# A list scheduler with other distances between engines, other GpSimd durations and other constants

## The chip, the core and the metric

The kernel runs on one core of a Trainium2 chip. The metric is the device time of one execution in microseconds (us). Of the kernel before, 15 runs are known, from 796.47 to 799.75, with a median of 798.31. One further execution was recorded by the hardware profiler.

The engines are named as in the profile: PE (TensorE, matrix products, with PEld for the loading of its weights), DVE (VectorE), ACT (ScalarE), POOL (GpSimd) and SP (SyncE, whose queue issues most of the DMA transfers). Each engine works through its own list of instructions in order. An instruction that isn't ready holds up all that stand behind it on its engine.

## The reference

Two layers run over x (4 sequences of 1024 tokens, 128 features), each with a layernorm over its sum with x:

```python
# selective state space layer: 256 channels, 16 states
xz = x @ W_in.T                       # xr, z
xs = silu(causal_conv(xr, 4 taps) + conv_b)
dt_r, b_sel, c_sel = split(xs @ W_x.T)
dt = softplus(dt_r @ W_dt.T + b_dt)
h  = exp(dt * a) * h + (dt * x_t) * b_t          # token after token
y  = sum_s h * c_t + D * x_t
x  = layernorm(x + (y * silu(z)) @ W_out.T)
# mixture of 8 experts, the best 2 of each token
scores = x @ Wr + br; weights = softmax(top 2)
out = sum over experts of weight * (gelu(x @ W1 + b1) @ W2 + b2)   # 128 -> 512 -> 128
x   = layernorm(x + out)
```

The program computes all of it in float32.

## The kernel before, in words

**Units and states.** The 4096 tokens are cut into ten units (`UNITS`, L42) of 256, 256, 512 (six times), 384 and 128 tokens, numbered 0 to 9. Each unit runs through 16 states s, and a state is one pass over the unit's tokens for all 256 channels, which lie as two halves c of 128 partitions. Here a state is called "S4.9" or "state 9 of unit 4". It takes these steps in `step`:

- PE spreads the column of B over the partitions (tile u, L824, at most 4 transposes);
- DVE multiplies, u = dtx * u (L861), and runs two scans along the tokens, h = a*h + u (L880, first c = 1, then c = 0);
- ACT makes a = exp(dt * nega) for the scans (L847, 7 buffers);
- POOL multiplies hc = h * cc, a half at a time (L895), and copies the last column of h as the state of the next unit of the same sequence (L920), where the sequence goes on. SP loads cc, the row of C for all partitions;
- PE adds hc, transposed, to y (L905).

h has 2 buffers, hc 3, cc 4. So the scan of a state waits until POOL has made hc of the state two before it.

**Around the states.** While unit i runs, `prepare(i+1)` makes the next one's xs, zs, dt and dtx (projections L585 to L721, DVE's q L753, dt L766, dtx L780). `finish_mixer` closes unit i during unit i+1: yg = y * zs on DVE (L959), transposes py on PE (L973) with copies yt on ACT (L980), the output projection po on PE (L991, L1002), the layernorm (stats_m L466 and mv_m L468 on DVE, rstd_m on ACT and DVE), the transposes pt_f (L1027) and the copy xf (L1031), the router's product pr (L1036), and on DVE the scores sc (L1057), the ranks (L1071 to L1077) and the weights rw (L1098 to L1101).

**Experts.** The tokens of a round (`ROUNDS`, L45: units 0 and 1, then each unit to 8 by itself, as rounds 0 to 7) are sorted by expert into blocks of 128 slots, 15 in a round, 13 in round 7. `dispatch` counts on PE (L1140, L1149), numbers the blocks on DVE (L1174 to L1193), finds each token's slot (L1202 to L1220) and its weight (L1233, L1241), and then POOL scatters the rows into `xs_slots` by indirect DMA (L1262), two for each 128 tokens: 8 of them, 6 in round 7. `experts` loads four blocks at a time (xb, L1332), transposes them on PE (pt_b, L1343), makes xq on ACT or DVE (L1350, L1359), multiplies by the expert's weights w (loaded by SP, L1402) on PE (L1290), takes the GELU on ACT (ht, L1303), multiplies by the second weights (L1314), weighs yb on ACT or DVE (L1426, L1428) and stores it (L1435). `combine` adds the biases (L1461, L1473), gathers the rows back on POOL (L1495), and does the last layernorm (stats_o L466, o L492) and the store (L1524). Unit 9 isn't sorted; all 8 experts run over its 128 tokens (`dense`, L1532 to L1564).

**What sets the order.** Nothing above is issued as it is written. Each operation is added to a `Plan` (L77 to L248) with an engine, a cost in us, what it reads and writes, a place (a due time) and an urgency. `order` is a list scheduler: on each engine it takes, among the operations that could start within NEAR of the earliest, that with the lowest place less urgency. An operation is known to be ready when all that it needs has ended, plus a hop when that ran on another engine (`HOP`, L81). Other rules: a buffer must be free; an ACT operation that needs another function table counts LOTH later than it could start, unless its urgency is RUSH, and 1.28 for the switch; DVE operations marked `port` and POOL's hc aren't planned at the same time; POOL's scatters and gathers (`beside`) are put next to DVE work by BESIDE and PATIENCE. What `order` returns is issued in that order on each engine, and `issue` adds a load of ACT's function table where the next operation needs another one (L243). The costs and places shape the order alone; on the chip each instruction starts when its engine and its data are there.

The places come from the constants of L19 to L40. `prepare` of unit i is due PREP + PREP_OF[i] before its start, the dispatch of round r at the end of its last unit plus D_AT + D_OF[r], the experts X_AT + X_OF[r], the combining C_AT + C_OF[r] behind. `finish_mixer` has the urgency URG, or RUSH in the last N_RUSH units (L952).

Of the kernel before, what the change touches and what calls it, by code (L numbers as in the profile page):

```python
# [16 lines left out]
NTC = T // P  # L17

RUSH = 100.0  # L19
NEAR, LOTH = 0.1, 1.3  # L20

UP = 0.95
GATHER, SCATTER = 1.85, 1.35
N_B = 2
SCAN_ORDER = 1, 0
B_AT, B_URG = 3.6, 29.9
BESIDE = -6.2
PATIENCE = 0.2
N_RUSH = 0
X_AT, X_STEP, X_URG, C_AT, C_URG, D_AT = 1.9, 2.66, 6.2, 4.0, -1.0, -1.9  # L30
A_AT, A_URG, BC_AT, BC_URG = -0.8, -2.3, 4.2, 15.8
PREP, SEL, SOFT, SSTEP = 25.4, 5.3, -0.1, 2.7
L_URG = -1.0
URG, URG2, URG3, URG4 = 52.0, 191.1, 18.3, 0.8
Z_AT, W2_AT, W1_AT, W1_STEP = 11.2, 0.0, 6.8, 3.5

PREP_OF = (-6.7, -1.0, -10.0, 9.5, 1.2, 0.0, -3.0, 5.6, -5.2, 6.9, -3.9, 3.0)
D_OF = (7.9, -3.5, -6.5, 3.3, 6.5, 4.7, -8.1, 5.3, 4.5, 1.7)
X_OF = (-1.9, -7.6, 2.1, 1.3, 0.5, 0.4, 0.8, -16.1, 6.0, -2.5)
C_OF = (-0.2, 5.0, -3.5, -1.3, 8.3, 3.3, 21.1, -2.6, 2.7, 9.1)  # L40

UNITS = [  # L42
    (0, 0, 256), (0, 256, 256), (0, 512, 512), (1, 0, 512), (1, 512, 512), (2, 0, 512), (2, 512, 512), (3, 0, 512), (3, 512, 384), (3, 896, 128),
# [33 lines left out]
class Plan:  # L77

    HOP = {"PE": 0.3, "DVE": 0.12, "ACT": 0.15, "POOL": 0.15}  # L81

    def __init__(self):
        self.ops, self.room, self.place = [], {}, 0.0
# [62 lines left out]
    def order(self, near=0.1, switch=1.28, loth=1.3, ahead=60.0, free_tags=("mm",)):  # L147
# [13 lines left out]
        while ready:  # L161
# [5 lines left out]
            for op in ready:  # L167
# [17 lines left out]
                if op["beside"] and needy:  # L185
                    if port[0] == "DVE" and max(t, port[1]) <= port[2] - BESIDE:
                        t = max(t, port[1])
                    else:
                        t = max(t, known + PATIENCE)
                s = t  # L190
# [61 lines left out]
def tile_mamba_moe_postln(  # L252
# [171 lines left out]
    def size(i):  # L424
        return UNITS[i][2], UNITS[i][2] // P
# [376 lines left out]
    def step(i, st, s):  # L802
        t_n, n = size(i)
        b, first, _ = UNITS[i]
        goes_on = i + 1 < NU and UNITS[i + 1][0] == b
        if s == 0 and first == 0:
            state[b] = sb(small, [P, NS, NDC], "state", 2, f"state_{b}")
        carry = state[b]
        place = plan.place
        cc = sb(scan, [P, T], "cc", 4, f"cc_{i}_{s}")  # L810
        cd, bt, dt, dtx = st["cd"], st["bt"], st["dt"], st["dtx"]
        turn = turns[0]
        bank = 2 * (turn % N_B)
        turns[0] += 1
        spreads[turn], users[turn] = [], []
        begun[turn] = plan.buf(None, 1, None)
        to_spread = lambda ins: apart(spreads[turn], ins, users.get(turn - 1, ()))
        to_use = lambda ins: apart(users[turn], ins, spreads.get(turn + 1, ()))
        row = plan.buf("row", N_B, lambda: u_sb[:, bank, :])

        def spread():
            for k in range(n):
                to_spread(
                    nc.tensor.transpose(  # L824
                        u_sb[:, bank, k * P : (k + 1) * P],
                        bt()[:, k, s : s + 1].to_broadcast([P, P]),
                        ident,
                    )
                )


        late = [begun[turn - 1]] if turn else []
        pe(0.12 * n, spread, [bt, *late], [row], place=place - B_AT, urgent=B_URG)
        dma(
            lambda: nc.sync.dma_start(
                out=cc()[:, :t_n], in_=cd()[s, :t_n].partition_broadcast(P)
            ),
            [cd],
            [cc],
            t_n // 2,  # L840
            place=place - BC_AT,
            urgent=BC_URG,
        )
        a = sb(scan, [P, NDC, T], "a", 7, f"a_{i}_{s}")
        act(
            2 * t_n,
            lambda: nc.scalar.activation(  # L847
                a()[:, :, :t_n], dt()[:, :, :t_n], AF.Exp, scale=nega[:, s : s + 1]
            ),
            [dt, decay],  # L850
            [a],
            EXP,
            place=place - A_AT,
            urgent=A_URG,
        )
        h = sb(scan, [P, NDC, T], "h", 2, f"h_{i}_{s}")

        dve(
            2 * t_n,
            lambda: to_use(  # L860
                nc.vector.tensor_tensor(  # L861
                    (u_sb[:, 1:3, :t_n] if bank else u_sb[:, 1::-1, :t_n]),
                    dtx()[:, :, :t_n],
                    u_sb[:, bank : bank + 1, :t_n].to_broadcast([P, NDC, t_n]),
                    ALU.mult,
                )
            ),
            [dtx, row],
            [u_first, row, begun[turn]],
            port=False,  # L870
        )
        hc = sb(scan, [P, NDC, T], "hc", 3, f"hc_{i}_{s}")
        if s == 0:
            add_skip(i, st)
        y = st["y"]
        for c in SCAN_ORDER:

            def run(c=c):
                to_use(
                    nc.vector.tensor_tensor_scan(  # L880
                        h()[:, c, :t_n],
                        a()[:, c, :t_n],
                        u_sb[:, (1, bank)[c], :t_n],
                        0.0 if first == 0 else carry()[:, s, c : c + 1],
                        op0=ALU.mult,
                        op1=ALU.add,
                    )
                )

            plan.add(  # L890
                "DVE", (0.21 if first else 0.15) + 2.1e-3 * t_n, run, [(u_first, row)[c], a] + [(carry, s)] * (first > 0), [(h, c)]
            )

            def times(c=c):
                nc.gpsimd.tensor_tensor(  # L895
                    hc()[:, c, :t_n], h()[:, c, :t_n], cc()[:, :t_n], ALU.mult
                )

            plan.add(
                "POOL", 0.05 + 2.33e-3 * t_n, times, [(h, c), cc], [(hc, c)], urgent=30.0, port=True  # L900
            )

            def add(c=c):
                for k in range(n):
                    nc.tensor.matmul(  # L905
                        y()[:, k, c * P : (c + 1) * P],
                        hc()[:, c, k * P : (k + 1) * P],
                        ident,
                        is_transpose=True,
                        start=False,  # L910
                        stop=(s == NS - 1),
                        skip_group_check=True,
                    )

            plan.add("PE", 0.12 * n, add, [(hc, c), y], [y], urgent=30.0)
        if goes_on:
            plan.add(
                "POOL",
                0.15,
                lambda: nc.gpsimd.tensor_copy(carry()[:, s, :], h()[:, :, t_n - 1]),  # L920
                [h],
                [(carry, s)],
                urgent=30.0,
            )
# [24 lines left out]
    def finish_mixer(i, st, at):  # L949
        t_n, n = size(i)  # L950
        plan.place = at
        plan.urgent = URG if i < NU - N_RUSH else RUSH  # L952
        yg = sb(tmp, [P, NTC, DI], "sq", 2, f"yg_{i}")
# [614 lines left out]
    for rd in rounds:  # L1568
        c = 0
# [99 lines left out]
```

## Time and profile before

| | |
|---|---|
| median of 15 runs | 798.31 us (796.47 to 799.75) |
| the profiled execution | 795.18 us |
| its span, first to last instruction | 793.5 us |
| mean granted TensorE clock | 0.913 |
| hc (L895), halves of 512 tokens | 192 of 1.428 us |
| state copies (L920) of this form | 96 of 0.342 us |
| first scans of 512 with a state / without | 1.266 / 1.208 us |
| u (L861) of 512 tokens | 1.227 us |
| ACT table loads (L243) | 105 of 1.283 us |
| rows gathered (L1495) | 62 of 1.579 us |

The page first gives the busy time of each engine, its share of the span and its instructions; then the span in 40 slices with the busy share in tenths. The table of waits names the waiting operation, what it waited for, and the sum, the number and the longest of the waits. A line of the timeline gives start, duration, engine, line, operation, tiles, and in brackets the idle time ahead of it with what ended it; the mean times in the table are those of groups of one shape. Idle time of an engine matters only where its work sets the end.

### The profile page before, as it was taken

What the parts mean: (1) busy time and instruction counts of PE and PEld (TensorE: products, weight loads), DVE (VectorE), ACT (ScalarE), POOL (GpSimd) and SP (SyncE); (2) the same over time, 40 slices, a digit from 0 to 9 for tenths busy, and PEclk for the clock granted to TensorE, in tenths of its full rate; (3) what the DMA queues carried; (4) which work ended last, traced back from release to release, by engine and by line L of the source; (5) the groups of instructions that cost most, each with busy time, mean ns of one, the idle gap of its engine ahead of it and who ended that gap; (6) DMA issues with size and microseconds to landing.
All of it is one profiled execution on the core that took longest, in us unless ns stands there. A gap on an engine that the chain in (4) does not pass through costs nothing. (4 is left out here: it accounts for less than half of the span.)

```text
span 793.5 us, 14284 instructions
## 1 busy us (share of the span) xinstructions
PE 657.4 (83%) x4594; PEld 561.5 (71%) x4594; DVE 656.5 (83%) x1036; ACT 557.8 (70%) x843; POOL 534.2 (67%) x637
## 2 busy tenths in 40 slices
PE   5557838669997999799987996899889988888786
PEld 4446526359875987598766874888678978777785
DVE  1698999999979998999989989999979997985322
ACT  3853855817867886778777888788867876676553
POOL 4356545576656897479938795869787886985604
PEclk9666958869997999899998998899989999999998
DMA  6962313347414664267524733556355555566652
GB/s 198 222 150 54 107 47 107 99 133 230 142 56 132 188 175 119 67 175 182 140 61 134 198 82 113 152 178 161 91 146 173 145 145 174 147 143 180 156 158 46
DMA packets 106120, 109.20 MB, mean 138 GB/s; under 512 B 9640, under 2 KB 72152, under 8 KB 106048
## 3 DMA queue, kind: packets, MB, share of 16 engines
q1 hardware_dynamic: 94384, 99.44, 44.3%
q0 software_dynamic: 11248, 8.33, 6.0%
q8 instruction: 38, 0.62, 0.3%
q10 hardware_dynamic: 416, 0.53, 0.3%
q14 instruction: 34, 0.28, 0.1%
HBM read 87.96 MB, written 18.27 MB: 134 GB/s over the span
## 5 line engine op out<-in xcount | busy, mean ns | idle before, releaser
L895 POOL TENSOR_TENSOR hc<-h,cc 128x512 f32<-128x512 f32 (+3 forms) x320 | 357.7, 1212 | 156.2 <-PE y L905 35.1
L905 PE MATMUL y<-ident,hc 128*128 128x128 f32 x1024 | 173.0, 293 | 48.3 <-POOL hc L895 45.8
L880 DVE TENSOR_TENSOR_SCAN h<-a,state,u 128x512 f32<-128x512 f32 (+3 forms) x192 | 185.4, 1000 | 20.5 <-POOL hc L895 7.3
L847 ACT ACTIVATE a<-dt,nega 128x1024 f32<-128x1024 f32 (+3 forms) x160 | 152.9, 974 | 66.5 <-DVE h L880 60.3
L861 DVE TENSOR_TENSOR u<-dtx,u 128x1024 f32<-128x1024 f32 (+3 forms) x160 | 162.2, 1014 | 22.0 <-PE u L824 9.5
L905 PEld LDWEIGHTS y<-ident,hc 128*128 128x128 f32 x1024 | 124.7, 150 | 77.3 <-POOL hc L895 71.3
L1314 PE MATMUL ph<-w_sb,ht 128*128 x944 | 131.6, 292 | 24.4 <-ACT ht L1303 24.2
L1314 PEld LDWEIGHTS ph<-w_sb,ht 128*128 128x128 f32 x944 | 121.6, 206 | 29.0 <-ACT ht L1303 28.6
L880 DVE TENSOR_TENSOR_SCAN h<-a,u 128x512 f32<-128x512 f32 (+1 forms) x128 | 132.9, 1075 | 10.1 <-POOL hc L895 3.6
L1290 PE MATMUL ph<-xq,w 128*128 128x128 f32 x944 | 125.9, 283 | 15.4 <-DVE pick L1233 3.2
L243 ACT ACT_TABLE_LOAD x105 | 134.7, 1283 | 3.6 <-PEq L1657 1.8
L1290 PEld LDWEIGHTS ph<-xq,w 128*128 128x128 f32 x944 | 116.3, 198 | 21.4 <-issue 6.4
L1495 POOL DMA_INDIRECT acc<-ys_slots,slot_i x62 | 97.9, 1579 | 39.2 <-DMA ys_slots<-yb 22.3
L824 PE MATMUL u<-ident,bt 128*128 128x128 f32 x512 | 89.3, 289 | 10.7 <-DVE h L880 10.7
L1303 ACT ACTIVATE ht<-ph 128x512 f32<-128x512 f32 x118 | 66.0, 597 | 23.5 <-PE ph L1290 22.6
L824 PEld LDWEIGHTS u<-ident,bt 128*128 128x128 f32 x512 | 65.1, 147 | 20.6 <-DVE h L880 13.1
L1426 ACT ACTIVATE yb<-ph,xb 128x128 f32<-128x128 f32 x105 | 37.2, 363 | 46.7 <-PE ph L1314 41.1
L1262 POOL DMA_INDIRECT xs_slots<-acc,slot_i x31 | 34.9, 1126 | 46.9 <-DVE twin L1241 13.2
L613 PE MATMUL pxc<-xt,taps 128*128 128x512 f32 (+3 forms) x160 | 60.2, 524 | 3.5 <-ACT xt L603 2.9
L613 PEld LDWEIGHTS pxc<-xt,taps 128*128 128x128 f32 x160 | 29.4, 199 | 24.8 <-issue 17.5
L745 ACT ACTIVATE sq<-ex,shift 128x1024 f32<-128x1024 f32 (+3 forms) x40 | 38.0, 973 | 7.3 <-DVE q L753 6.8
L1262 POOL DMA_INDIRECT xs_slots<-twin,slot_i x31 | 35.7, 1151 | 6.7 <-issue 5.4
(140 smaller groups left out, 706.3 us busy)
## 6 DMA issues: line engine op xcount, KB each, us to landing
w<-w_dram SPq DMA_DIRECT2D x118, 256.0 KB
cc<-cd SPq DMA_DIRECT2D x96, 256.0 KB
xb<-xs_slots SPq DMA_DIRECT2D x24, 258.0 KB
ys_slots<-yb SPq DMA_DIRECT2D x24, 256.0 KB
cc<-cd SPq DMA_DIRECT2D x32, 128.0 KB
cc<-cd SPq DMA_DIRECT2D x16, 192.0 KB
w_sb<-in_w_dram SPq DMA_DIRECT2D x8, 256.0 KB
w_own<-in_w_dram SPq DMA_DIRECT2D x8, 256.0 KB
```

Of the source, the lines that this page charges most:

```text
L243: load(table)
L613: nc.tensor.matmul(pp()[:, :t_n], taps[:, k, c * P : (c + 1) * P], xt()[:, k : k + t_n], start=(k == 0), stop=(k == KC - 1),)
L824: nc.tensor.transpose(u_sb[:, bank, k * P : (k + 1) * P], bt()[:, k, s : s + 1].to_broadcast([P, P]), ident,)
L847: lambda: nc.scalar.activation(a()[:, :, :t_n], dt()[:, :, :t_n], AF.Exp, scale=nega[:, s : s + 1]),
L861: nc.vector.tensor_tensor((u_sb[:, 1:3, :t_n] if bank else u_sb[:, 1::-1, :t_n]), dtx()[:, :, :t_n], u_sb[:, bank : bank + 1, :t_n].to_bro ...
L880: nc.vector.tensor_tensor_scan(h()[:, c, :t_n], a()[:, c, :t_n], u_sb[:, (1, bank)[c], :t_n], 0.0 if first == 0 else carry()[:, s, c : c + 1],
L895: nc.gpsimd.tensor_tensor(hc()[:, c, :t_n], h()[:, c, :t_n], cc()[:, :t_n], ALU.mult)
L905: nc.tensor.matmul(y()[:, k, c * P : (c + 1) * P], hc()[:, c, k * P : (k + 1) * P], ident, is_transpose=True, start=False, stop=(s == NS - 1),
L1262: ins = nc.gpsimd.indirect_dma_start(out=rd["xs"]()[:, :], out_offset=bass.IndirectOffsetOnAxis(ap=slot_i()[:, k, st["chunk"] + c : st["ch ...
L1290: nc.tensor.matmul(ph()[:, k * P : (k + 1) * P], w()[:, k * P : (k + 1) * P], xt()[:, width], start=True, stop=True, skip_group_check=True,)
L1314: nc.tensor.matmul(py, ht[:, k, :], w2_sb[:, bass.ds(e, 1), k * DM : (k + 1) * DM].rearrange("p o d -> p (o d)"), start=(k == 0), stop=(k ...
L1495: nc.gpsimd.indirect_dma_start(out=acc()[:, c, :DM], out_offset=None, in_=ys()[:, :], in_offset=bass.IndirectOffsetOnAxis(ap=slot_i()[:, k ...
```

## The change

No operation, buffer or dependence is changed. The scheduler's figures are: the hops between engines, POOL's cost of an hc and of a state copy, and nearly all constants that give places, urgencies and the rules for tables and for POOL beside DVE. So the orders on all five engines differ, and the number of ACT table loads, 105 before, is 90 after.

```diff
-NEAR, LOTH = 0.1, 1.3
+NEAR, LOTH = 0.1, 1.6
-GATHER, SCATTER = 1.85, 1.35
+GATHER, SCATTER = 1.65, 1.25
-B_AT, B_URG = 3.6, 29.9
-BESIDE = -6.2
-PATIENCE = 0.2
-N_RUSH = 0
-X_AT, X_STEP, X_URG, C_AT, C_URG, D_AT = 1.9, 2.66, 6.2, 4.0, -1.0, -1.9
-A_AT, A_URG, BC_AT, BC_URG = -0.8, -2.3, 4.2, 15.8
-PREP, SEL, SOFT, SSTEP = 25.4, 5.3, -0.1, 2.7
-L_URG = -1.0
-URG, URG2, URG3, URG4 = 52.0, 191.1, 18.3, 0.8
-Z_AT, W2_AT, W1_AT, W1_STEP = 11.2, 0.0, 6.8, 3.5
+B_AT, B_URG = 5.3, 30.0
+BESIDE = -13.6
+PATIENCE = 0.3
+N_RUSH = 2
+X_AT, X_STEP, X_URG, C_AT, C_URG, D_AT = -1.0, 2.33, 6.9, 4.9, -0.5, 0.9
+A_AT, A_URG, BC_AT, BC_URG = 4.5, 0.2, 2.6, 24.4
+PREP, SEL, SOFT, SSTEP = 25.3, 7.2, 2.6, 3.6
+L_URG = -2.0
+URG, URG2, URG3, URG4 = 49.9, 241.6, 23.0, 3.7
+Z_AT, W2_AT, W1_AT, W1_STEP = 38.1, -3.2, 2.2, 7.5
-PREP_OF = (-6.7, -1.0, -10.0, 9.5, 1.2, 0.0, -3.0, 5.6, -5.2, 6.9, -3.9, 3.0)
-D_OF = (7.9, -3.5, -6.5, 3.3, 6.5, 4.7, -8.1, 5.3, 4.5, 1.7)
-X_OF = (-1.9, -7.6, 2.1, 1.3, 0.5, 0.4, 0.8, -16.1, 6.0, -2.5)
-C_OF = (-0.2, 5.0, -3.5, -1.3, 8.3, 3.3, 21.1, -2.6, 2.7, 9.1)
+PREP_OF = (-6.7, -0.5, -10.6, 3.4, 0.9, -0.2, -3.0, 1.4, -1.9, 4.2, -9.5, 5.6)
+D_OF = (6.1, -9.1, -5.7, 8.1, 5.3, -0.2, -2.2, 9.8, 4.6, 1.2)
+X_OF = (-1.9, -7.6, 8.3, 5.3, -1.3, 2.1, -4.0, -13.7, 11.7, -0.1)
+C_OF = (-0.1, 19.3, -4.2, 0.4, 8.5, 2.2, 12.4, -1.7, 2.7, 9.3)
-    HOP = {"PE": 0.3, "DVE": 0.12, "ACT": 0.15, "POOL": 0.15}
+    HOP = {"PE": 0.5, "DVE": 0.15, "ACT": 0.3, "POOL": 0.6}
-                "POOL", 0.05 + 2.33e-3 * t_n, times, [(h, c), cc], [(hc, c)], urgent=30.0, port=True
+                "POOL", 0.08 + 2.4e-3 * t_n, times, [(h, c), cc], [(hc, c)], urgent=30.0, port=True
-                0.15,
+                0.32,
```

## The prediction

> **What bounds the kernel now.** I read the page's busy times first, then the slices, the instruction groups, the waits of DVE, the windows of the end, and last the timelines of DVE, POOL and PE around single waits.
>
> ```profile
> PE 657.4 (83%) x4594; PEld 561.5 (71%) x4594; DVE 656.5 (83%) x1036; ACT 557.8 (70%) x843; POOL 534.2 (67%) x637
> ...
> DVE  1698999999979998999989989999979997985322
> ```
>
> DVE's row of slices tells three stretches. It is low for about 29 us (loads and the first projection; the first u starts at 29.31), then 8 or 9 nearly throughout, then it falls after 715. In the long middle DVE sets the pace: a state of 512 tokens is one u (1.23 us) and two scans (1.27 + 1.21), which with gaps comes about every 4.1 us. So there time comes only from DVE's idle.
>
> ```profile
> DVE h L880 <- POOL hc L895: 10.9, 3, 6.4
> ...
> DVE u L861 <- PE u L824: 9.5, 9, 3.3
> ...
> DVE sc L1057 <- PE pr L1036: 4.8, 4, 3.0
> DVE h L880 <- POOL state L920: 3.8, 2, 3.4
> DVE stats_m L466 <- PE po L1002: 3.4, 3, 2.0
> ```
>
> These waits of DVE (us, times, longest) are what a new order can remove. Before 714.9 the timeline of DVE holds 9.0 of the u waits (one of 0.29 comes later, the rest are smaller than 0.2), 4.8 + 3.4 = 8.2 for the new layernorm and router, 1.0 for a gathered acc, and 3.59 + 0.85 + 3.36 + 0.5 on POOL: some 26 us. The larger waits of the view (yb, acc, q) lie in the end or the head.
>
> ```profile
> 714.90:735.50 20.60, 17.82 (x134) 15.28 (x134) 10.48 (x37) 12.19 (x28) 10.62 (x21) 1.00 0.65 176
> 735.50:793.50 58.00, 43.64 (x360) 41.29 (x360) 15.59 (x62) 28.00 (x50) 21.70 (x14) 0.95 0.49 119
> ```
>
> These are windows of the end (length, then busy PE, PEld, DVE, ACT, POOL, clock). From the last dispatch (L1174, 714.88) to the last instruction is 78.6 us: 20.67 until the first block of round 7 is transposed (pt_b, 735.55), then 58 of a PE chain, round 7's 13 blocks and 8 dense ones. **So the time is where the last dispatch stands, plus the end behind it.**
>
> **The change, part by part.** No operation changes; only the orders do, and with them the ACT table loads, 105 before and 90 after. The steps are counted in the two listings of each engine's order, priced by rows of before. The constants, the hops (HOP) and the two GpSimd costs are the scheduler's figures and cost no time on the chip. The profiled run took 795.18, its span was 793.5 (1.7 lies around it), 3.1 under the median of 798.31. I sum on the span and add 4.8 at the end.
>
> (1) *Table loads*: 15 x 1.283 (L243) = 19.2 us less on ACT. ACT is 70% busy and DVE waits for it once, for 10.2 in the head, where the order is nearly the same. I take 0 here; the other engines' waits on ACT are in terms 3 and 7. The next ACTIVATE starts as a load ends (the load at 695.50 ends at 696.78, the next starts at 696.80). The Trainium skill ("ScalarE: Activation LUTs", What ACT_TABLE_LOAD costs) adds a drain to each load, about 2.7 us in all; by that estimate ACT would save 40 us, and the sum would be the same.
>
> (2) *The last dispatch stands later.* Before, it follows both scans of state 10 of unit 9; after, it stands between the two scans of state 15. The same router operations stand ahead of it in both. Added ahead of it: u and scans of states 11 to 14, u and one scan of 15. A state of this unit comes every 1.52 us (u at 695.51, 697.03, 698.55), the last part is 0.43 + 0.10 + 0.47: 4 x 1.52 + 1.0 = **+7.1**. It is certain as work, as these states otherwise run behind the dispatch, where they are hidden.
>
> (3) *Router and projection waits* (8.2). PE and ACT work between them is unchanged, but DVE's own work between yg and stats_m, and from mv_m to sc, grows: in unit 5 from 8.1 to 12.1 and 7.0 to 12.4, in unit 4 to sc 7.5 to 10.7. The longest waits are 3.0 and 2.0, so most are covered; unit 2's stretch to sc shrinks (8.4 to 6.8) and unit 8's to stats_m (7.3 to 6.0). Bounds -8.2 and 0; I take **-6**, near the covered end.
>
> (4) *u waits* (9.0). Spreads (L824) move earlier on PE: 53 of 160 had two whole states of y still behind them, now 77. But lumps stay: up to 8.3 us of PE work ahead of one spread after, 5.4 at the longest wait of before (3.34). Bounds -9 and +3 (one more such wait); I take **-4**. The acc wait goes: **-1**.
>
> (5) *Scatters.* GpSimd runs the 8 scatters of a round in one block, and h has two buffers, so the scan two states on waits for the hc behind the block.
>
> ```profile
> 591.04 2.33 DVE L880 TENSOR_TENSOR_SCAN h<-a,u 128x512 f32<-128x512 f32 x2 [3.59 <-POOL hc L895]
> ```
>
> This is round 5's block (577.27 to 589.7, then 1.24 for the hc). DVE work between the last L1241 and the waiting scan was 11.4 there, 10.2 in round 6 (waited 3.36), and 14.6 or more in all rounds before them, without a wait. After: 15.3, 14.6, **7.5**, 14.7, 15.0, 10.1, 7.8. Demand is 0.4 to 1.7 to start, 10.2 to 12.4 for the block, 1.3 for one hc: 12 to 15. Round 2 gets a new wait, 7.5 against 13 = 5.5 (4.8 to 6.3); round 5 keeps about 3.6; round 6 goes from 3.4 to 4.9. **+7**, bounds 0 (scatters fall between hc after all) and +8.
>
> The skill ("SBUF — State Buffer", Who interferes with whom) says that DVE operations with two SBUF inputs lock out GpSimd's reads. In this trace a scatter takes 0.96 to 2.03, and the block took 10.2 while DVE stood and up to 12.4 while it worked. By that rule a wait would shorten its own block, and +7 would be nearer +5 (the two blocks are 2.2 apart). It speaks against any fixed duration for GpSimd, which the new costs are too.
>
> (6) *Unit 8's yg* (L959) comes after, directly behind its last scan with only 1.1 us of DVE work between; hc and y need about 3: **+2** (0 to 2.5). Nine gathers now stand among unit 9's states, 1.58 each beside hc: **+0.5** (0 to 1).
>
> (7) *The end.* The stall after the last scatters goes (only half a scan follows them):
>
> ```profile
> 720.15 1.04 POOL L1262 DMA_INDIRECT xs_slots<-acc,slot_i  x1 [6.41 <-DVE h L880]
> ...
> 728.53 0.85 DVE L880 TENSOR_TENSOR_SCAN h<-a,state,u 128x128 f32<-128x128 f32 x2 [6.42 <-POOL hc L895]
> ```
>
> The block ends at 727.60, 12.7 behind the dispatch; xb's loads are issued from 730.11 to 733.76, and the first pt_b at 735.55 stands behind y, yg and py. After: 3.4 for the dispatch, 0.4 to 1.7, 7.45 for 6 scatters, 2.5, 3.65, under 1: 17.5 to 19 instead of 20.7, **-2.5** (-4 to 0). On SP, xb's first load stands behind the weights of round 7's first five blocks, in before behind those of six. PE must fill it: 21 expert blocks stood behind the last y, now 28 or 29. The extra 7.5 of round 6 at some 2.1 (16 matmuls of 2.05, with the transpose) are 16 us, which fit. Behind pt_b_0 three blocks are issued ahead of their second layers, and a store moves ahead of the last dense expert: **-1** (-2.5 to +1).
>
> Sum: 7.1 - 6 - 4 - 1 + 7 + 2 + 0.5 - 2.5 - 1 = **+2.1**. Span 795.6, at the median 798.3 + 2.1 = 800.4; I say **800**.
>
> **Rivals.**
> *A: the waits on PE vanish (the other side: faster).* The order now counts 0.5 instead of 0.3 behind each PE result, so DVE work stands ahead of L1057, L466 and L861. For it speaks the longer work in (3); against it, the lumps in (4). With all 18.2 gone: 7.1 - 18.2 + 7 + 2 + 0.5 - 2.5 - 1 = -5.1, so 793.2; I say **793**. My forecast leaves 7.2 of the 18.2; the sign turns where less than 5.1 is left.
> *B: PE falls behind (slower by more).* The 7.5 deferred blocks stand in the window of the last dispatch, where DMA is busy 0.65; xb's load waits on SP for weight buffers that come free only as PE ends round 6. Then pt_b_0 and the end gain nothing (+3.5), and the lumps keep the u waits (+4): 2.1 + 3.5 + 4 = +9.6, **808**. It decides from 2.5 us a block: 7.5 x 2.5 = 18.8, past the window of 18.
> *C: the losses cancel*: the orders lose the same in other places, within 1.6 of before, **798**. For it speaks that no single term above is over 1%.
>
> **How the numbers follow.** Forecast (797 to 805, losses shifted, a little slower): 0.40; A (785 to 797): 0.32; B (805 to 813): 0.20; C lies between the first two, 0.08. By the bounds of (3) to (7) the sum could fall by 2.2 + 5 + 7 + 2 + 0.5 + 1.5 + 1.5 = 19.7 or rise by 6 + 7 + 1 + 1 + 0.5 + 0.5 + 2.5 + 2 = 20.5 if all were on one side. They are independent, so I take half of each around 800.4, 790.5 to 810.6, and widen to **789 to 811** for waits that no row shows; that leaves out the outer ends of A and B, about 0.2. 1.6 us (0.2%) is about what can be told from no change: 796.7 to 799.9 counts as the same. Faster: A and 0.06 of the forecast, 0.38. Same: C and 0.05 of the forecast, 0.13. Slower: the other 0.29 of the forecast and B, 0.49. Terms of both signs cancel here, so the sign is weakly held; the forecast's own range is 797 to 805.
>
> **What would show it.** In the profile after: L1174 of the last dispatch near 720 (714.9 + 7.1 - 11 + 9.5 = 720.5); DVE waits on POOL hc of 5 us at state 9 of unit 4, and near 4 and 5 in the rounds 5 and 6; sc and stats_m waits under 2.5 together; u waits near 5; DVE's wait of 6.42 near the end gone; pt_b_0 about 18 behind L1174; then 57 to the end. I am wrong if round 2's scatters interleave with hc, if spreads wait behind the lumps more than before, or if PE is late with round 6.

## The result and the profile after

The changed kernel takes 817.82 us (median of 8 runs, 815.74 to 821.05), the kernel before 797.68 (40 runs, 794.89 to 800.64). The ratio is 1.0253 [1.0237, 1.0268]: 20.1 us slower. The direction was that of the forecast. The size was not: 2.1 us were forecast, and the time lies above the range of 789 to 811.

Of the kernel after there are three profiles, with spans of 818.3, 814.8 and 812.6; their mean, 815.2, is 21.7 above the 793.5 of before's profile. Where one number is given for after, it is the mean of the three, with their spread. In two of the groups of runs (e1, e2, e3 and e5; e6, e7, e8 and e10) before itself takes 810 and 808, at a granted clock of 0.90 instead of 0.91, so every ratio goes with the runs of before from the same group. Some expectations below put this down to the chip; the record has its chip number 3 both beside 810 and, in a later group, beside 798, so that is not shown.

The page of the first profile of after: engine busy times with instruction counts, and DVE's slices.

```profile
PE 665.7 (81%) x4594; PEld 566.1 (69%) x4594; DVE 663.7 (81%) x1036; ACT 539.1 (66%) x828; POOL 529.9 (65%) x637
...
DVE  1798899999788999798999999998997996872322
```

DVE's shape is the same, low, full, and falling behind the last dispatch. Only the full stretch is longer. ACT is 18.7 less busy, as 15 loads fewer say (90 of 1.283), and the kernel is slower. One number should surprise: DVE executes the same 1036 instructions and is busy for 663.7 instead of 656.5 (661.0 and 661.9 in the other two profiles).

The waits of DVE in the same profile (us in total, times, longest):

```profile
DVE h L880 <- POOL state L920: 11.9, 4, 5.3
DVE u L861 <- PE u L824: 11.5, 12, 2.2
DVE yg L959 <- PE y L905: 10.7, 2, 9.6
...
DVE h L880 <- POOL hc L895: 6.1, 5, 4.8
...
DVE stats_m L466 <- PE po L1002: 3.2, 3, 1.7
DVE sc L1057 <- PE pr L1036: 2.2, 4, 0.7
DVE rstd_m L480 <- ACT rstd_m L474: 1.2, 1, 1.2
DVE xt L590 <- PE po L991: 1.2, 1, 1.2
```

The two POOL rows together have gone from 14.7 (with 6.4 of it behind the last dispatch) to 18.0, all of it ahead of the dispatch. The waits for sc shrank, but rstd_m and xt appear in their stead. The u waits didn't shrink (12 times here, 10 and 8 in the other two profiles, 9 before). Of the yg row, 9.6 stand in the end.

Windows of the end (length, then busy PE, PEld, DVE, ACT, POOL, clock, DMA share): from the last L1174 to the first pt_b of round 7, and from there to the last instruction.

```profile
738.60:757.65 19.05, 16.39 (x135) 14.94 (x134) 4.41 (x23) 9.94 (x21) 6.80 (x12) 1.00 0.61 180
757.65:818.30 60.65, 44.62 (x357) 42.25 (x355) 15.97 (x63) 28.81 (x55) 21.74 (x14) 0.91 0.49 121
```

The last L1174 starts at 738.60 instead of 714.88; the end behind it takes 79.7 (78.0 and 76.7 in the other two profiles) against 78.6. **So nearly all of the loss lies ahead of the last dispatch, in DVE's full stretch.** Its account, from DVE's timeline up to the last L1174 (waits of 0.2 and more by what ended them; router means sc, stats_m, rstd_m and xt):

| | before | after, three profiles | difference of the mean |
|---|---|---|---|
| last L1174 at | 714.9 | 738.6, 736.8, 735.9 | +22.2 |
| DVE busy ahead of it | 630.4 | 643.3, 640.7, 641.6 | +11.5 |
| of that, work moved ahead (5 u of 0.43, 9 scans of 0.467) | | | +6.4 |
| waits for POOL | 8.3 | 17.9, 18.1, 19.1 | +10.1 |
| waits for u | 9.0 | 11.5, 11.0, 8.3 | +1.3 |
| router waits | 8.2 | 7.2, 6.5, 7.7 | -1.1 |
| other waits (yg, ACT, acc, a scan behind its u) | 1.1 | 2.4, 2.0, 2.3 | +1.2 |
| head and gaps under 0.2 | 57.9 | 56.3, 58.6, 56.9 | -0.7 |

**The scatter waits.** DVE's timeline of after (start, duration, line, tiles, and the idle ahead with what ended it) has them in rounds 1, 2, 5 and 6:

```profile
261.12 2.33 DVE L880 TENSOR_TENSOR_SCAN h<-a,u 128x512 f32<-128x512 f32 x2 [2.48 <-POOL state L920]
...
343.10 2.45 DVE L880 TENSOR_TENSOR_SCAN h<-a,state,u 128x512 f32<-128x512 f32 x2 [4.79 <-POOL hc L895]
...
629.79 2.33 DVE L880 TENSOR_TENSOR_SCAN h<-a,u 128x512 f32<-128x512 f32 x2 [3.66 <-POOL state L920]
...
688.78 1.92 DVE L880 TENSOR_TENSOR_SCAN h<-a,state,u 128x384 f32<-128x384 f32 x2 [5.34 <-POOL state L920]
```

Together they are 16.3, against 7.0 in rounds 5 and 6 of before. And POOL's timeline shows round 2's block, from its first scatter to the hc behind it, as forecast:

```profile
331.86 1.04 POOL L1262 DMA_INDIRECT xs_slots<-acc,slot_i  x1 [3.49 <-DVE twin L1241]
...
341.79 6.18 POOL L895 TENSOR_TENSOR hc<-h,cc 128x512 f32<-128x512 f32 x5
```

The block ends at 341.8, the first hc 1.24 later at 343.0, and the scan starts at 343.10.

**The longer DVE operations.** By shape, a few small groups of DVE have other means than before: L1071 0.998 us (before 0.410), L1101 0.706 (0.313), L753 of 768 elements 1.817 (0.950). The timelines show why a mean can double: single instructions stretched to several times their length.

```profile
493.39 3.00 DVE L1071 TENSOR_TENSOR gt<-sc 128x256 f32<-128x256 f32 x1
496.31 0.41 DVE L1072 TENSOR_TENSOR eq<-sc 128x256 f32<-128x256 f32 x1
```

Beside the first of them on POOL in the same profile:

```profile
491.76 4.33 POOL L895 TENSOR_TENSOR hc<-h,cc 128x512 f32<-128x512 f32 x3
```

L1072 is of the same shape and form as L1071 and takes 0.41. The long one starts while POOL multiplies and ends at 496.39, when POOL's run of hc ends (496.09). An L1101 of 2.57 (0.19 elsewhere) starts at 577.54 and ends at 580.11, POOL's hc beside it at 580.05. Before has such cases too (an L1073 of 2.67 at 476.61, beside a gather and an hc that ends at 478.98), but fewer: 13 that take at least 0.4 us more than the shortest of their shape, 14.4 us in all, against 18 and 19.4 in this profile. Each of these 31 overlaps an hc. L1071 and L1101 read two operands from SBUF. The Trainium skill ("SBUF — State Buffer", Who interferes with whom) says of such operations that they and GpSimd's reads exclude one another for a whole instruction; the rows agree in kind, with 3.00 instead of 0.41, but this operation was held over more than one hc (1.43 in the mean). An L1076, with one tensor to read, was held too: 2.02 instead of 0.18 at 644.23 in before. The experiment e7 below moves hc against an unchanged order of DVE, and the stretches move with them.

### The profile page after: what moved, and what is told of

It reads as the page before. It is cut to its first block, busy times and chain, and to the rows that moved or that the text cites. A ratio compares the mean times of both kernels' runs of the same rounds, so it can differ in the third digit from the quotient of the medians.

```text
span 818.3 us, 14298 instructions
## 1 busy us (share of the span) xinstructions
PE 665.7 (81%) x4594; PEld 566.1 (69%) x4594; DVE 663.7 (81%) x1036; ACT 539.1 (66%) x828; POOL 529.9 (65%) x637
## 5 line engine op out<-in xcount | busy, mean ns | idle before, releaser
L895 POOL TENSOR_TENSOR hc<-h,cc 128x512 f32<-128x512 f32 (+3 forms) x320 | 353.7, 1191 | 165.1 <-PE y L905 45.8
L905 PE MATMUL y<-ident,hc 128*128 128x128 f32 x1024 | 168.3, 294 | 43.2 <-POOL hc L895 41.3
L861 DVE TENSOR_TENSOR u<-dtx,u 128x1024 f32<-128x1024 f32 (+3 forms) x160 | 162.2, 1014 | 23.2 <-PE u L824 11.5
L905 PEld LDWEIGHTS y<-ident,hc 128*128 128x128 f32 x1024 | 124.2, 150 | 70.2 <-POOL hc L895 64.0
L1290 PE MATMUL ph<-xq,w 128*128 128x128 f32 x944 | 129.7, 289 | 21.9 <-DVE pick L1233 6.4
L1314 PE MATMUL ph<-w_sb,ht 128*128 x944 | 130.9, 291 | 15.2 <-ACT ht L1303 14.9
L1290 PEld LDWEIGHTS ph<-xq,w 128*128 128x128 f32 x944 | 120.1, 203 | 27.0 <-issue 10.3
L1314 PEld LDWEIGHTS ph<-w_sb,ht 128*128 128x128 f32 x944 | 121.2, 204 | 21.0 <-ACT ht L1303 19.2
L1495 POOL DMA_INDIRECT acc<-ys_slots,slot_i x62 | 99.6, 1607 | 49.5 <-DVE acc L1555 23.8
L824 PE MATMUL u<-ident,bt 128*128 128x128 f32 x512 | 91.7, 295 | 24.3 <-DVE h L880 24.0
L1262 POOL DMA_INDIRECT xs_slots<-acc,slot_i x31 | 33.0, 1065 | 52.4 <-ACT dt L721 10.9
L745 ACT ACTIVATE sq<-ex,shift 128x1024 f32<-128x1024 f32 (+3 forms) x40 | 38.1, 974 | 10.8 <-DVE q L753 10.2
L753 DVE SCALAR_TENSOR_TENSOR q<-sq,q 128x1024 f32<-128x1024 f32 (+3 forms) x30 | 36.2, 1207 | 2.1
```

What stands on the lines that cost most here:

```text
L824: nc.tensor.transpose(u_sb[:, bank, k * P : (k + 1) * P], bt()[:, k, s : s + 1].to_broadcast([P, P]), ident,)
L861: nc.vector.tensor_tensor((u_sb[:, 1:3, :t_n] if bank else u_sb[:, 1::-1, :t_n]), dtx()[:, :, :t_n], u_sb[:, bank : bank + 1, :t_n].to_bro ...
L895: nc.gpsimd.tensor_tensor(hc()[:, c, :t_n], h()[:, c, :t_n], cc()[:, :t_n], ALU.mult)
L905: nc.tensor.matmul(y()[:, k, c * P : (c + 1) * P], hc()[:, c, k * P : (k + 1) * P], ident, is_transpose=True, start=False, stop=(s == NS - 1),
L1290: nc.tensor.matmul(ph()[:, k * P : (k + 1) * P], w()[:, k * P : (k + 1) * P], xt()[:, width], start=True, stop=True, skip_group_check=True,)
L1314: nc.tensor.matmul(py, ht[:, k, :], w2_sb[:, bass.ds(e, 1), k * DM : (k + 1) * DM].rearrange("p o d -> p (o d)"), start=(k == 0), stop=(k ...
```

## The experiments

### The two halves of the change

Only the figures (hops and the two POOL costs) put into before, only the constants put into after's place, and a very small change of one figure:

```
e1_costs_only = before +             e2_constants_only = after with
  HOP of after                         HOP of before
  hc cost 0.08 + 2.4e-3 * t_n          hc cost 0.05 + 2.33e-3 * t_n
  state copy 0.32                      state copy 0.15
c1_hop_a_little = before with HOP["PE"] 0.32 instead of 0.3
```

> The kernel before with the new hops and the two new GpSimd costs, all constants as before. Theory 1 (the time goes where the order puts the dispatches: DVE work left behind the scatters, and the place of the last dispatch): DVE work behind the scatters is 7.0, 9.0, 8.9 and 5.6 us in rounds 2, 4, 5 and 6 in this order, so at a demand of about 13 they wait some 5 + 4 + 4 + 6.5 = 19 instead of 7, and the last dispatch stands behind all of state 15 (+8): 798 + 12 + 8 = about 818. Rival (durations and hops nearer to the trace give the better order, and only the new constants are bad): 798 or less.

> The kernel after with the hops and the GpSimd costs of before, so the new constants alone. Theory 1: DVE work behind the scatters is 6.8, 10.5 and 6.5 us in rounds 2, 3 and 6: about 5 + 3 + 6 = 14 instead of 7, the last dispatch at state 13 (+4), some 3 for longer DVE operations: 798 + 14 = about 812. Rival (the new hops and costs make the loss): back near 798.

> The kernel before with PE's hop at 0.32 instead of 0.30 and nothing else; from the middle of the program on the order differs. The scatters keep their cover (DVE work within 1.3 of before in each round) and the last dispatch stands one state earlier. Theory 3 (the constants are fitted to the exact figures, so any new figure costs per cents): 1 to 4% slower. Rival (only a different place of dispatches and scatters matters): within 0.7% of before.

Measured: figures alone 876.5, ratio 1.0826 [1.0787, 1.0864]; constants alone 878.1, ratio 1.0838 [1.0798, 1.0878]; the small hop 799.5, ratio 1.0029 [1.0016, 1.0042].

Each half alone loses three times what both lose together, so the loss isn't the sum of a good half and a bad one, and neither theory holds in size. In both, the last L1174 comes late (773.2 and 770.3) and the end takes long, 99.7 and 108.3 instead of 78.6, at a mean granted clock of 0.81 and 0.80. So figures and constants act together; that the constants were fitted to the figures suits this, and is not tested. Most of what these two lose ahead of the last dispatch wasn't followed up; in e1 the largest new item is DVE's wait for the biases (acc L1473, 22.2 in 3 waits; in before 0.4 in the whole run). That any new figure costs per cents does not hold for the small step of the third run, which loses 0.3%.

### The last dispatch by itself

```diff
# e5_before_last_dispatch_late: before, with the last dispatch (and all that needs it)
# taken out of its place and put between the scans of state 15, as after has it
-    order = plan.order(NEAR, loth=LOTH)
+    order = later(plan, plan.order(NEAR, loth=LOTH), dispatched[7], scans[9, 15, 0])
# e6_after_last_dispatch_sooner: after, with the last dispatch alone moved behind state 12
+    order = pulled(plan, plan.order(NEAR, loth=LOTH), dispatched[7], scans[9, 12, 0])
```

> The kernel before, with only the last dispatch (and what needs it) moved from behind state 10 of the last unit to between the two scans of its state 15, as in the kernel after. Theory 1: +7.1 of DVE work ahead of the dispatch, and 1.6 given back between dispatch and first block as the stall behind the scatters goes: +5.5, so about 803.5. Rival (the stall was as long as the states that are moved, so nothing is lost): 798 within 1.6.

> The kernel after, only the last dispatch moved from between the scans of state 15 of the last unit to behind those of state 12 (its weights are ready there). Theory 1: 2.65 states of 1.52 are no longer ahead of it, -4.0; the stall behind the scatters comes back and the first block stands 1.6 later behind the dispatch: -2.4, 2.3% above before.

Measured: in before, the later dispatch costs 1.0105 [1.0054, 1.0155], that is +8.5 us [4.4, 12.6]. In after, the earlier dispatch makes it worse, 845.9, ratio 1.0472 [1.0436, 1.0508].

In e5's profile DVE is busy for 637.6 ahead of the last L1174, 7.2 more than in before, which bears out step (2) as work. The interval of the time holds the +5.5 expected and much else: the u waits were 23.8 in this run, and no profile of before from the same group shows how many of them the group brings. The run e6 is a lesson on experiments rather than on the dispatch: only the dispatch moved, while PE kept its order, so PE stood for the y behind the scatter block:

```profile
762.90 0.47 PE L905 MATMUL y<-ident,hc 128*128 128x128 f32 x1 [10.33 <-POOL hc L895]
```

Behind that idle time 8 matmuls (L1314, at 763.16) take 1.91, where 16 take 2.05 at the full clock. (After itself wasn't run in this group, so the 1.0472 is compared with ratios of 1.025 to 1.027 from others.)

### Taking the scatter waits away

A third buffer for h (a buffer less for xf pays for it). In after the planner's own counts stay at two and three, so its orders are unchanged; the same edit in before. The kernel e3 was run in the first of the two groups named above, and again, as e3b, beside after itself.

```diff
-        h = sb(scan, [P, NDC, T], "h", 2, f"h_{i}_{s}")
+        h = plan.buf("h", 2, lambda: scan.tile([P, NDC, T], F32, tag="h", name=f"h_{i}_{s}", bufs=3))
-        xt = sb(io, [P, T], "xf", 3, f"xf_{i}")
+        xt = plan.buf("xf", 3, lambda: io.tile([P, T], F32, tag="xf", name=f"xf_{i}", bufs=2))
```

> The kernel after, all five orders the same, with three buffers of h instead of two (and two of xf instead of three, to make room), so that a scan waits for hc of three states before. Theory 1: the four waits of 2.5, 4.8, 3.7 and 5.3 us behind scatters shrink by up to a state each (4.1, or 3.1 of 384 tokens): -2.5 - 4.1 - 3.7 - 3.1 = -13, and most of it reaches the end: 805 to 810. Rival (POOL and PE behind it set the pace there, the waits come back at y, yg or u): 815 or more.

> The kernel after as it is, so that the kernels with three buffers of h can be compared with it on one chip. It should stand 2.5% above before, as in its first runs.

> The kernel after with three buffers of h, again, now beside the kernel after itself: before, it stood 3.6% above the kernel before on a chip on which that one took 810. Theory 2, formed after that run (PE is as late as POOL; a DVE that needn't wait for hc runs ahead and then waits for its spread u, or for y at the end): DVE's waits on POOL go from 18 to under 3, those on u rise by 10 or more, and the time is within 1% of the kernel after. Theory 1 (the scatter waits are lost time): 10 us or more below the kernel after.

> The kernel before, the same orders, with three buffers of h (two of xf). Theory 1: the waits of 3.6 and 3.4 behind the scatters of rounds 5 and 6 go, -6, so 0.8% less than before. Theory 2: the u waits take their place, within 0.3% of before.

| | us | ratio to before | waits for POOL | waits for u |
|---|---|---|---|---|
| after, same group as the next two | 818.1 | 1.0273 [1.0224, 1.0323] | 18.1 | 11.0 |
| e3b, after with three h | 812.7 | 1.0192 [1.0162, 1.0223] | 2.7 | 20.4 |
| e4, before with three h | 795.1 | 0.9981 [0.9965, 0.9997] | 0.7 | 15.1 |
| e3, the same kernel as e3b, other group | 837.0 | 1.0356 [1.0309, 1.0404] | 0.5 | 38.9 |

The POOL waits go, and only a third of them comes back as time: 5.4 of 15.4 in after, 2.1 of 7.6 in before. The intervals of the ratios are wide against this: for before they allow 0.2 to 2.8 of the 7.6, so the third is rough. The rest turns into waits for u. So theory 2 holds in the sums: e3b is 0.7% below after, and e4 0.2% below before. After with three h, the place of the old 4.79:

```profile
343.13 1.23 DVE L861 TENSOR_TENSOR u<-dtx,u 128x1024 f32<-128x1024 f32 x1 [2.39 <-PE u L824]
...
349.18 1.23 DVE L861 TENSOR_TENSOR u<-dtx,u 128x1024 f32<-128x1024 f32 x1 [2.27 <-PE u L824]
```

Where DVE stood for 4.79 it now stands for 2.39 and 2.27. What holds the spreads there is PE's own work. PE's timeline of e3b up to the first of them:

```profile
337.10 2.05 PE L1290 MATMUL ph<-xq,w 128*128 128x128 f32 x16 [0.78 <-DVE acc L1473]
...
340.71 1.95 PE L1314 MATMUL ph<-w_sb,ht 128*128 x16
342.49 0.60 PE L824 MATMUL u<-ident,bt 128*128 128x128 f32 x4
```

From 337.10 to the second of these spreads, which ends at 349.15, PE has no idle time. So the larger part of what the scatter blocks took would have been lost on the spreads in any case. e4 is the one kernel here that beats both, by 0.19%, with an interval that reaches to 0.03%. e3 is within 1.6 us of e3b from 385 to 613 us and falls behind from there; why stays open, and with 1.0356 and 1.0192 for the same kernel a ratio from one group can't be set against one from another to better than some 1.6%.

Letting ready hc run between the scatters, by POOL's order alone (a reordering of its list behind `order`: each hc goes ahead of the first operation that starts, by the plan, when it is ready; units 1 to 8):

```diff
+    order = mixed(plan, plan.order(NEAR, loth=LOTH), times_ops)
```

> The kernel before with the same change of POOL's order as the kernel e8 has. Theory 2: POOL waits of 8 fall to 1 or 2 and u stays: -5, 0.6% faster than before. Rival (longer blocks, later experts): slower than before by up to 1%.

> The kernel after, only POOL's order changed: in units 1 to 8 an hc that is ready by the plan goes between the scatters of a block instead of behind them. Theory 2 (behind the block PE's y is late, with it the next spread, so a third h alone moved the wait from POOL to u): now y is not late, POOL waits fall from 18 to under 5 without u rising, -10: 1.4% above before. Rival (the block becomes longer by the hc in it, some 5 to 8 us, so the experts of each round start later and PE idles): no gain, 2.5% or more above before.

Measured: before so mixed 817.7, ratio 1.0115 [1.0092, 1.0138]; after so mixed 834.2, ratio 1.0313 [1.0277, 1.0349]. The rival is near the time in before; in after there is no gain either, though 1.0313 isn't clear of after's ratios from other groups. The block is broken up, but it takes longer: 13.6 to 16.4 in rounds 1 to 6 of the two, but for one of 11.7 and one of 12.4, against 10.2 to 12.4 in before and 9.9 to 12.6 in after. The waits for POOL go from 8.3 to 5.9 in before and rise to 24.1 in after.

The larger part is on DVE, and the rival didn't name it. DVE's order is the same as in before, but its busy time ahead of the last L1174 goes from 630.4 to 640.5 (to 650.2 in after). One of its operations in before and in e7, and POOL beside it in e7:

```profile
584.36 0.96 DVE L766 SCALAR_TENSOR_TENSOR dt<-q,dt 128x768 f32<-128x768 f32 x1
```

```profile
601.58 3.29 DVE L766 SCALAR_TENSOR_TENSOR dt<-q,dt 128x768 f32<-128x768 f32 x1
601.54 2.50 POOL L895 TENSOR_TENSOR hc<-h,cc 128x512 f32<-128x512 f32 x2
```

Of DVE's instructions ahead of the last dispatch, 16 take over 0.3 more in e7 than in before, 16.6 in all, and 15 of these lie beside an hc; 6 take less, 6.6 in all, and all 6 lay beside an hc in before. The L1076 of 2.02 is one of these: no hc is beside it in e7, and it takes 0.18. The net of 9.9 is about the loss of 9.3, though other waits moved too (u from 9.0 to 14.4). So with POOL's order alone changed, the stretches go where the hc go. The block as a whole is the better of the two.

### The places of the dispatches, and the end

In after, round 5's dispatch stands in state 12 of unit 7 (before: state 6), since slot_i has two buffers and round 3's gathers hold one. A third slot_i lets the planner put it back. Two further variants take some constants of before.

```diff
# e10_after_three_slot_i, e10b_after_three_slot_i
-        slot_i = sb(small, [P, TOPK, MAXC], "slot_i", 2, f"slot_i_{r}", U32)
+        slot_i = sb(small, [P, TOPK, MAXC], "slot_i", 3, f"slot_i_{r}", U32)
# v30_last_dispatch_planned
+A_AT, A_URG, BC_AT, BC_URG = -0.8, -2.3, 4.2, 15.8
# v25_dispatches_earlier
+B_AT, B_URG = 3.6, 29.9
```

> The kernel after with three buffers of slot_i instead of two, planned anew: the order is the same up to unit 7, where round 5 is dispatched at state 6 instead of 12, as it no longer waits for the gathers of round 3; round 6 at state 10 of unit 8 instead of 8, round 7 at state 13 of unit 9 instead of 15. Theory 4 (a dispatch that comes late leaves PE without blocks, and the blocks pile up at the end): PE's idle time between the dispatches of rounds 4 and 5 falls from 18.9 to about 12, the last dispatch comes 2 states (3 us) earlier, the cover of round 5's scatters is 7.3, 2 us more of waiting: -8, so 1.7% above before. Rival (DVE's own waits decide, and these don't change): within 0.4% of the kernel after.

> The kernel after as it is, as the control for the three others: 2.5 to 2.7% above before on a chip where before takes 797; more, perhaps 3.5%, where before takes 808.

> The kernel e10 again, beside the kernel after: three buffers of slot_i, round 5 dispatched at state 6 of unit 7. Theory 4: below the kernel after by 1%. What e10 showed on the other chip (an end of 114 us with PE at half its clock): above it by 2% or more.

> The kernel after with only A_AT, A_URG, BC_AT and BC_URG (due times of the exponentials and of the loads of cc) as before; planned anew, the order is the same up to state 6 of unit 8, and the last dispatch stands at state 12 instead of 15 of unit 9. Theory 1 (the last dispatch's place carries its DVE work to the end): 2.65 states fewer ahead, -4.6, +1.6 between dispatch and first block: 3 us (0.4%) below the kernel after. Rival (PE's backlog of blocks of round 6 sets the end): no gain.

> The kernel after with only B_AT and B_URG (due times of the spreads) as before; the same order up to state 12 of unit 4, then round 5 is dispatched at state 6 instead of 12 of unit 7, and round 7 at state 12 instead of 15 of unit 9. Theory 4 (late dispatches leave PE without blocks and pile them up): the 4.2 us of DVE work less ahead of the last dispatch, and some 6 of PE idle less in unit 7: 8 to 10 us (1.1%) below the kernel after. Rival (the body's waits decide): within 0.5% of it.

| | us | ratio to before | last L1174 | end behind it |
|---|---|---|---|---|
| after, again | 816.7 | 1.0246 [1.0225, 1.0267] | 735.9 | 76.7 |
| v25 | 824.9 | 1.0351 [1.0329, 1.0372] | 733.1 | 86.5 |
| v30 | 845.8 | 1.0615 [1.0592, 1.0638] | 738.3 | 103.2 |
| e10b | 850.4 | 1.0657 [1.0614, 1.0699] | 741.5 | 114.0 |
| e10, other group | 860.8 | 1.0673 [1.0636, 1.0709] | | |

That an earlier place of the dispatches wins the loss back is refuted for these orders. The last L1174 stays within 6 us of after's, and time is lost behind it, 10 to 37 us. In e10b a part of this is work: 584 matmuls stand behind its last L1174, 490 behind after's (500 in v25, 502 in v30). Two windows of v30's end:

```profile
738.31:778.31 40.00, 31.44 (x240) 28.63 (x239) 13.18 (x53) 22.12 (x44) 16.18 (x22) 0.96 0.55 149
786.00:816.72 30.72, 23.95 (x89) 19.68 (x90) 4.28 (x15) 6.77 (x13) 0.00 (x0) 0.50 0.21 64
```

The clock column falls from 0.96 to 0.50, and PE is busy 23.95 with 89 matmuls, 0.269 each, where 240 took 31.44 ahead of it, 0.131 each. PE's timeline shows where it starts:

```profile
781.60 2.05 PE L1314 MATMUL ph<-w_sb,ht 128*128 x16
786.83 1.12 PE L1343 MATMUL pt_b<-ident,xb 128*128 128x128 f32 x4 [3.18 <-DVE yb L1428]
```

PE idles 3.18, and from there 4 transposes take 1.12 (0.60 in after's end). The Trainium skill ("TensorE: Matmul & The Clock Gate", What's actually happening) says that TensorE drops to half its clock after an idle window of some 3.4 us, and that busy time brings it back. Here it dropped within an idle time of 3.18 and stayed low for 30.7 us of a chain whose matmuls are parted by short waits. A full idle window isn't needed in this case: in after's end the clock is 0.50 from 780.60 to 784.01, and the longest idle time of PE just ahead is 1.34. Nor does such an idle time alone keep it low: behind one of 3.16 at 326.99 in after, it is 0.50 for 3.4 us only. Over their ends, before and after both keep 0.91 or more in the mean. So these ends are long with a PE that runs at half clock for 38.5 us of v30's, 38.6 of e10b's and 37.9 and 44.1 of e1's and e2's (7.6 to 10.4 in after). In v30 PE is busy 15 us longer in the end than in the last profile of after, and idle 11 longer. What keeps the clock low there was not tested.

### Whether PE's load makes the u and router waits

In rounds 0 to 5 the second layer of the experts (L1314) does one of its four matmuls; the outputs of these experts are left incomplete. Orders and all other work are unchanged.

```diff
-                second_layer(py()[:, :DM], e(), ht())
+                second_layer(py()[:, :DM], e(), ht(), NPC if r > 5 else 1)
```

> The kernel before, the same orders, but the experts of rounds 0 to 5 multiply only one of the four parts of their second layer (three of four matmuls of L1314 are left out there, so the experts' output is not the reference's): PE has some 90 x 3 x 0.13 = 35 us less to do ahead of the last dispatch, the end is the same. Theory 5 (PE is as loaded as DVE, and a wait of DVE on u, po or pr is PE's backlog): these waits fall from 17 to under 7, the last dispatch comes 10 earlier: 1.2% faster. Rival (they come from the distance between the engines, a fixed latency): within 0.4% of before.

> The kernel after with the same matmuls left out in rounds 0 to 5. Theory 5: waits on u, po and pr fall from 16 to under 7, those on POOL stay near 18, the last dispatch comes 9 earlier: 1.3 to 1.5% above the unchanged kernel before, still 20 above the kernel p1 at its last dispatch. Rival: 2.5% above before, as the kernel after.

Measured: before with less PE work 797.9, ratio 1.0004 [0.9981, 1.0026]; after with less 815.1, ratio 1.0221 [1.0195, 1.0247]. The page of p1:

```profile
PE 629.4 (79%) x4054; PEld 515.5 (65%) x4054; DVE 656.8 (82%) x1036; ACT 556.0 (70%) x843; POOL 532.2 (67%) x637
```

540 matmuls are gone, PE is busy for 28 us less, and nothing comes of it: the u waits are 9.3 ahead of the last dispatch (9.0 before), the router's 10.1 (8.2). In after they are 8.7 and 6.5. The wait for pr that took 3.01 at 316.6 in before takes 2.99 at 317.6. So the experts' second layer doesn't make these waits, and theory 5, a general backlog of PE, falls.

That doesn't clear PE's work of them. The longest u wait of before, first PE's timeline, then DVE's:

```profile
222.22 7.04 PE L613 MATMUL pxc<-xt,taps 128*128 128x512 f32 x16
229.10 0.60 PE L1027 MATMUL pt_f<-ident,acc 128*128 128x128 f32 x4
229.53 0.60 PE L824 MATMUL u<-ident,bt 128*128 128x128 f32 x4
```

```profile
230.17 1.23 DVE L861 TENSOR_TENSOR u<-dtx,u 128x1024 f32<-128x1024 f32 x1 [3.34 <-PE u L824]
```

The spread stands behind 16 matmuls of the next unit's projection and 4 transposes, and PE doesn't pause. Nor does it elsewhere: of the 17.2 us that DVE stands for u, po and pr in waits of 0.2 and more ahead of before's last dispatch, PE is busy in all but 0.04, with projections, transposes, y, po, pr and the spreads themselves, and in none with L1314, the matmuls that p1 leaves out. In after PE is busy in all of the 17.5 us too (1.9 of them L1314). So these waits are PE work that stands directly ahead of what DVE needs, and the experiment took away other work. An order that cuts the projections into smaller parts, or a lighter projection, was not tried; nor were three h and a lighter PE together, where 4.4 of 26.3 us of such waits in e3b are L1314.

## Why the forecast was wrong, step by step

| step | forecast | measured (mean of three profiles) |
|---|---|---|
| (1) table loads | 0 | 0.6 more waits on ACT, no gain |
| (2) last dispatch | +7.1 | +6.4 as DVE work; +8.5 [4.4, 12.6] by e5, the end included |
| (3) router waits | -6 | -1.1 (-0.5 to -1.7) |
| (4) u waits | -4 | +1.3 (-0.7 to +2.5) |
| (4) acc | -1 | -1.1 |
| (5) scatters | +7 | +10.1 (9.6 to 10.8) |
| (6) yg, gathers | +2.5 | +1.1 for yg |
| other small waits, head, gaps | 0 | +0.4 |
| DVE operations stretched | not in the sum | +5.1 (3.9 to 6.6) |
| (7) the end | -3.5 | -0.5 (-1.9 to +1.1) |
| sum | +2.1 | +21.7 |

(In the last column (1) is a part of the other small waits, and for (2) the 6.4 is summed.)

Where the sum failed: steps (3) and (4) booked 11 us of waits on PE (and on acc) as gone, and 0.9 went; the stretch of DVE's operations beside hc, +5.1, was put at nothing; step (5) was 3.1 too small, and of step (7)'s gain of 3.5 only 0.5 came.

- **Step (3) failed in its logic.** "DVE's own work between ... grows, so most are covered" took each wait by itself. The waits for sc did shrink, from 4.8 to 2.2, as the step put it. But others took their place (rstd_m 1.2, xt 1.2, stats_m unchanged). The chain from yg to sc goes from DVE to PE and ACT and back several times, and DVE is in order: with more DVE work between two of its members the next member comes later, and a wait that is covered at one link can appear at another. That reading suits the rows and was not tested. What the rows do show is that PE is busy all through these waits, with po, pr and projections.
- **Step (4) went by the wrong count.** More spreads with two whole states of y still behind them (77 for 53) did not mean fewer waits: +1.3 instead of -4. By PE's rows, what decides is what stands directly ahead of the spread, and that is the lumps of PE work that the step named and allowed too little for. At the longest wait of before PE works without a pause for the 7.3 us from 222.22 to the spread, where the step had 5.4; after keeps waits behind the projections of the same unit (2.18 at 227.87) and of unit 7 (1.94 at 567.06). Rival A, all 18.2 gone, is wrong for the same reason. Rival B has the right sign and half of the mechanism: the lumps do keep the u waits, as it said, but round 7's first pt_b is on time, 19.07 behind L1174, and PE isn't late with round 6. Rival C, the losses cancel, fell with the forecast.
- **Step (5) had the mechanism, and was too small.** Rounds 2, 5 and 6 waited 4.79, 3.66 and 5.34 (forecast 5.5, 3.6, 4.9). Round 1 was called safe with 14.6 of cover against a demand of 12 to 15, and waited 2.48: DVE's work behind its last L1241 lasted from 245.58 to 258.64, 13.1, its block ran from 245.88 to 258.44, 12.6, and a state copy stands behind the hc. The bound of +8 was too tight: it was built from the rounds forecast to wait. The rule that the step drew from the skill had the direction for some blocks (9.9 in round 2, where DVE stood for 4.79, 12.6 in round 1, where it stood for 2.48), though before's round 5 took 12.4 with a wait of 3.59; and the sum went up from +7, not down to the +5 worked out by it.
- **Not counted: DVE operations stretched beside POOL.** The forecast gave the moved work by its rows and left the rest of DVE's busy time alone. With orders that put more small DVE operations beside hc, +5.1 net came from the same instructions, and e7 shows that the hc make it. Rows of before showed the effect (2.67 for 0.42 at 476.61), and it was not looked for.
- **Step (7) was right in direction.** The 6.42 stall is gone; L1174 to pt_b went from 20.67 to 19.07 in all three profiles, against a forecast of 18. What was gained there was in part lost in the chain behind it (57.9 before, 57.7 to 60.6 after).
- **Steps (1), (2), the acc and (6) held** within 1.5 us.

The sum of the terms was the wrong kind of sum. Its losses were work and buffers, and they came; its gains were waits that "are covered", and they didn't. e3b and e4 measured a rate, for the waits on POOL: what was taken off DVE there gave back about a third. By an estimate at a third, the gains of (3) and (4) would have been 3.7 instead of 11, and the forecast's sum +9.4. The rest of the miss is that these waits weren't taken off at all, the scatters' 3 us, the end's 3 and the 5 of the stretched operations. That the direction came out is in part luck: the sum rested on gains of 11, of which 0.9 came.

What stays open: how far another order of PE's projections would shorten the waits for the spreads, and how much of the +5.1 a plan could avoid.

## What to carry to other kernels

Book added work and added buffer waits in full, but a removed wait on an in-order engine at a fraction, until the next link of the same chain is shown to be early; here about a third came back. When an engine waits for another, first look in the trace whether that other one works or stands during the wait, and at which line: an experiment that takes other work off it says little. Where a reorder leaves instruction counts the same, still look for single instructions in the trace that take several times their usual time, and ask which engine they stood beside. And in a scheduler whose constants were fitted to its cost figures, don't judge a more truthful figure without refitting: here each half alone lost 8%, though a shift of one hop by 0.02 lost only 0.3%.

## What the runs showed of the hardware that was not expected

- A DVE operation of 0.41 us took 3.00 beside POOL's hc, one of 0.19 took 2.57; with POOL's order alone changed (e7), DVE's instructions ahead of the last dispatch took 9.9 us more.
- Within an idle time of 3.18 us on PE the granted clock fell to 0.50, and it stayed there for 30.7 us of a chain with short waits (4 transposes 1.12 instead of 0.60); behind another of 3.16 it was 0.50 for 3.4 us only.
- Less PE work lowered the mean granted clock, from 0.913 to 0.891, and the remaining y matmuls (L905) took 305 ns instead of 293.
